# A selective scan on one core: softplus in one activation, states carried as the scan's initial value, and seven of 24 C products on GpSimd

## The chip, the core and the metric

The kernel runs on one core of a Trainium2 chip. The core has five engines, each with its own in-order queue: TensorE (PE, matmuls; PEld is its weight load), VectorE (DVE), ScalarE (ACT), GpSimd (POOL) and SyncE (SP), which here issues nearly all DMAs. They meet in the on-chip memories SBUF (128 partitions) and PSUM (TensorE's output[...]), and wait for one another through semaphores. The metric is the device time of one execution in microseconds (us), the median of several.

## What is computed

Two images of 96 channels and 128x128 pixels pass through two layers. Layer 0 normalizes over channels, adds a four-direction Mamba block, and adds a small feed-forward network (FFN); layer 1 adds a 3x3 convolution and another FFN. Nearly all time is spent in the Mamba block. For each direction, with 192 inner channels, 16 states and 16384 tokens:

```
xz = x @ in_w.T;  xc, z = split(xz)
xc = silu(causal_conv4(xc) + conv_b)
dt_raw, B, C = split(xc @ xproj_w.T)          # 6, 16, 16 columns
dt = softplus(dt_raw @ dt_w.T + dt_b)
h[t] = exp(dt[t] * A) * h[t-1] + dt[t] * B[t] * xc[t]     # per channel, 16 states
y[t] = sum_s h[t, s] * C[t, s] + Dp * xc[t]
out = (y * silu(z)) @ outp_w.T
```

The four outputs are brought back to image order, concatenated, and multiplied by `fuse_w`.

## The kernel before

For each of two images (the loop at L607) there are three stages: `normalize`, `mamba` and `ffn_and_conv`. The change touches only `mamba`.

**Tiling.** The four directions are two pairs: forward over rows with forward over columns, then the two reversed ones. One pair has 2 x 192 = 384 inner channels, that is three groups g of 128 partitions (group 1 holds half of each direction). Tokens go in tiles of T = 512, so a pair has 32 tiles; with two pairs that is 64 steps per image, 128 in all. Inside a step the states are taken two at a time: a unit is (g, s), with g in 0..2 and s in 0, 2, .., 14, which makes 24 units, numbered 0 to 23. Two neighbouring units share a four-state tile of B rows and one of C rows, called quads here: 12 of each per step.

**What a unit does.**

- ScalarE makes the decay factors: two exponentials exp(A_s * dt) of 128x512, written to PSUM (`decay`, L364).
- GpSimd multiplies a whole quad of B rows, broadcast to 128 partitions by DMA, by dt*xc, in place (`b_part`, L354). It then adds what enters this tile from the one before to the first token of each state: `enter` = exp(A * dt[first token]) * last state (L320, L357, L358).
- VectorE runs two scans along the 512 tokens, h = da*h + b, from 0.0 (L368), one instruction each.
- The scan's result is multiplied by the C rows, 128x1024, in place of C (the C product). VectorE does this for most units (L456). For the units in `BY_POOL`, (0,8), (1,0) and (1,4), GpSimd does it (L375); then the scan writes into the B tile in SBUF, which GpSimd can read, instead of the decay tile in PSUM.
- ScalarE copies the two last columns of h to `hst`, the states that the next step starts from (L457).
- TensorE adds the products over the states into one PSUM tile y per group, by matmuls with the identity (`sums`, L372). At the end of a group VectorE multiplies y by silu(z) (`gated`, L379), and `project` adds the result to the output.

**Order.** All five queues are written out by hand (`in_order`). The loop at L484 has one iteration per unit k. In it stand, in this order: at even k the DMA of the B quad of unit k+6 (`fetch`) and the `b_part` of unit k+2 (`feed`); the tasks planned for (k, 0); scan 0 of unit k; then `behind(k-1)`, with the C product, state copy and sums of the unit before; the decay factors of unit k+2; scan 1 of unit k; at even k the DMA of the C quad of unit k+4; the tasks planned for (k, 1). For a unit in `BY_POOL` the product is issued one iteration later, at (k+1, 1), and its sums three later, at (k+3, 1). B has four quad buffers, C three, the decay factors three tiles, the y tile and the `misc` tile of PSUM one each.

**The next step's preparation** is spread over the units of the current one by `prologue`: a list `at` of (unit, before or after the scans, function). It holds the input DMA, the three in-projection groups with the convolution as four shifted matmuls (`conv`), silu of xc and of z (each one activation of 128x1536 with a table load before and behind it, L261 and L262), the matmul for dt_raw, B and C (`rows`), and the dt chain of each group. That chain writes softplus(v) as max(v,0) + log(1 + exp(-|v|)) with a correction term: six activations of 128x512 on ScalarE (Abs, Relu, Exp, Identity, Ln, Identity: L291 to L302) and three 128x512 operations on GpSimd (L305, L308, L311), then dt*xc on GpSimd (`dt_u`, L315).

Of the kernel before, what the change touches and what calls it, by code (L numbers as in the profile page):

```python
# [10 lines left out]
F32 = mybir.dt.float32  # L11
# [3 lines left out]
AF = mybir.ActivationFunctionType  # L15
ALU = mybir.AluOpType
# [7 lines left out]
T = 512  # L24
NT = L // T
R = T // W
S = 16
# [4 lines left out]
NG = 3  # L32
B_AHEAD = 3
C_AHEAD = 2
AHEAD = 2
BY_POOL = ((0, 8), (1, 0), (1, 4))
BCO = 32
NBC = 4 * S

# [2 lines left out]
def tile_metaformer(ctx: ExitStack, tc: tile.TileContext, a: dict, out: bass.AP):  # L42
    nc = tc.nc

    cpool = ctx.enter_context(tc.tile_pool(name="const", bufs=1))
# [14 lines left out]
    minus_one = cpool.tile([128, 1], F32, name="minus_one")  # L60
    nc.vector.memset(minus_one, -1.0)
    ident = const("ident", (128, 128))
    acc = accp.tile([C, L], F32, name="acc")
    blk = 4 * T
# [13 lines left out]
    dtb = const("dtb", (128, 2, NG))  # L78
# [4 lines left out]
    amat = cpool.tile([128, 2, NG, S], F32, name="amat")  # L83
# [103 lines left out]
    def mamba(acc, xnr, xnc):  # L187

        with ExitStack() as st:
            pool = lambda n, bufs, **kw: st.enter_context(tc.tile_pool(name=n, bufs=bufs, **kw))  # L190

            io, gen, one, mixp, two = (pool(*p) for p in (("io", 2), ("gen", 4), ("one", 1), ("mixp", 1), ("two", 2)))
# [1 line left out]
            rows_d = pool("rows_d", 3, space=DRAM)  # L194

            hst = one.tile([128, NG, S], F32, name="hst")
            enter = one.tile([128, NG, S], F32, name="enter")
            acc_w = acc.rearrange("c (h w) -> c w h", w=W)

            def misc():  # L200
# [15 lines left out]
            def prologue(pi, i, d):  # L216

                rev = pi == 1
                lo = L - (i + 1) * T if rev else i * T
                src = []  # L220

                def load():
                    for n, dram in (("xa", xnr), ("xb", xnc)):
                        t = io.tile([C, T + 3], F32, name=n)
                        if i == 0:
                            nc.gpsimd.memset(t[:, T : T + 3] if rev else t[:, 0:3], 0.0)
                            queue = nc.sync if rev else nc.gpsimd
# [4 lines left out]
                    d["dt"], d["dtu"], d["yg"] = [], [], []  # L232

                def conv(g):
                    d["ps"] = inproj(pi, g, lambda dd, k, lo, hi: inx[:, dd, k, lo:hi], src, (0, 1, 2, 3))
# [49 lines left out]
                    w = dtw[:, pi, g * 128 : (g + 1) * 128]  # L285
                    nc.tensor.matmul(d["ps"], w, d["rows"][0 : 2 * RK, :], start=True, stop=True)

                def dt_exp(g):
                    bias = dtb[:, pi, g : g + 1]
                    e = d["e", g] = one.tile([128, T], F32, name="e")  # L290
                    nc.scalar.activation(e, d["ps"], AF.Abs, bias=bias)  # L291
                    dt = gen.tile([128, T], F32, name="dt")
                    nc.scalar.activation(dt, d["ps"], AF.Relu, bias=bias)
                    nc.scalar.activation(e, e, AF.Exp, scale=-1.0)
                    d["dt"].append(dt)

                def dt_ln(g):
                    d["q"] = one.tile([128, T], F32, name="q")
                    nc.scalar.activation(d["q"], d["e", g], AF.Identity, bias=1.0)
                    d["ln"] = one.tile([128, T], F32, name="ln")  # L300
                    nc.scalar.activation(d["ln"], d["q"], AF.Ln)
                    nc.scalar.activation(d["q"], d["q"], AF.Identity, bias=minus_one[:, 0:1])  # L302

                def dt_q(g):
                    nc.gpsimd.tensor_tensor(d["q"], d["e", g], d["q"], ALU.subtract)  # L305

                def dt_log(g):
                    nc.gpsimd.tensor_tensor(d["ln"], d["ln"], d["q"], ALU.add)  # L308

                def dt_sum(g):  # L310
                    nc.gpsimd.tensor_tensor(d["dt"][g], d["dt"][g], d["ln"], ALU.add)  # L311

                def dt_u(g):
                    dtu = gen.tile([128, T], F32, name="dtu")
                    nc.gpsimd.tensor_tensor(dtu, d["dt"][g], d["xc"][:, g, :], ALU.mult)  # L315
# [17 lines left out]
                for g, ks in enumerate(((14, 15, 16, 18), *dts)):  # L333
                    at += [(k, 0, partial(f, g)) for k, f in zip(ks, (dt_in, dt_exp, dt_ln))]
                    at += [(ks[3] - 1, 1, partial(dt_q, g))]
                    at += [(ks[3] + m, 0, partial(f, g)) for m, f in ((1, dt_log), (1, dt_sum), (2, dt_u))]
                    if i > 0:
                        at += [((20, 24, 29)[g], 1, partial(entry, g))]

                outs = (conv_out, gate_out, rows_out, dt_exp)  # L340
# [9 lines left out]
                nc.sync.dma_start(t, src[None].broadcast_to((128 // n, n, 4, T)))  # L350
                return t

            def b_part(i, d, g, s, b):
                nc.gpsimd.tensor_tensor(b, d["dtu"][g][:, None, :].broadcast_to((128, 4, T)), b, ALU.mult)  # L354
                if i > 0:
                    if s == 0:
                        nc.gpsimd.tensor_tensor(enter[:, g, :], enter[:, g, :], hst[:, g, :], ALU.mult)  # L357
                    nc.gpsimd.tensor_tensor(b[:, :, 0], b[:, :, 0], enter[:, g, s : s + 4], ALU.add)  # L358

            def decay(pi, d, g, s):  # L360

                da = ps_w.tile([128, 2, T], F32, name="da")
                for j in range(2):
                    nc.scalar.activation(da[:, j, :], d["dt"][g], AF.Exp, scale=amat[:, pi, g, s + j : s + j + 1])  # L364
                return da

            def scan(j, da, b, h):
                nc.vector.tensor_tensor_scan(h[:, j, :], da[:, j, :], b[:, j, :], 0.0, ALU.mult, ALU.add)  # L368

            def sums(s, y, c):  # L370
                for j in range(2):
# [26 lines left out]
            steps = [(pi, i) for pi in range(2) for i in range(NT)]  # L398
            units = [(g, s) for g in range(NG) for s in range(0, S, 2)]
            nu = len(units)  # L400
            total = nu * len(steps)
            state = [{} for _ in steps]
            todo = {}

            def later(k, where, rank, f, *args):
                todo.setdefault((k, where), []).append((rank, partial(f, *args)))

            def issue(k, where):
                for _, f in sorted(todo.pop((k, where), ()), key=lambda p: p[0]):
                    f()  # L410
# [17 lines left out]
            bs, cs, das, hs, quads = {}, {}, {}, {}, {}  # L428
# [8 lines left out]
            def feed(k):  # L437

                if k < total:
                    n = k // nu  # L440
                    b_part(steps[n][1], state[n], *units[k % nu], quads.pop(k))

            def feed_decay(k):
                if k < total:
# [5 lines left out]
            def behind(k):  # L450
# [3 lines left out]
                h, c = hs.pop(k), cs.pop(k)  # L454
                if (g, s) not in BY_POOL:
                    nc.vector.tensor_tensor(c, h, c, ALU.mult)  # L456
# [27 lines left out]
            for k in range(total + 6):  # L484
                n, u = divmod(k, nu)
                if u == nu - 3:

                    prepare(n + 2)
                if k % 2 == 0:
                    fetch(k + 2 * B_AHEAD, 0, B_AHEAD, bs)  # L490
                    feed(k + AHEAD)
                issue(k, 0)
                if k < total:
                    (g, s) = units[u]
                    da, b = das.pop(k), bs.pop(k)
                    hs[k] = b if (g, s) in BY_POOL else da
                    scan(0, da, b, hs[k])
                if 0 < k <= total:
                    behind(k - 1)
                feed_decay(k + AHEAD)  # L500
                if k < total:
                    scan(1, da, b, hs[k])
                if k % 2 == 0:
                    fetch(k + 2 * C_AHEAD, 1, C_AHEAD, cs)
                issue(k, 1)
# [178 lines left out]
```

## Time and profile before

| what | us |
|---|---|
| median of three runs (11809.09 to 11811.6) | 11809.75 |
| profiled execution, its span | 11811.5 |
| of it, the 128 Mamba steps, by the spacing of L379 (81.17 each) | about 10390 |
| DVE busy in one step | 79.7 |
| POOL busy in one step | 77.6 to 79.3 |
| PE busy in one step | 72.7 |
| ACT busy in one step | 61.0 |

The profile's own execution took as long as the median of the runs, so sums made against it hold for the median. The rest, some 1420 us, is the normalization, the FFN and convolution stages and the filling of the pipeline; the change leaves their code alone.

In a group line of the profile, the numbers after the bar are the total busy time, the mean duration of one instruction in ns, then how long the engine stood idle just before such instructions and what ended most of that idle time. A reported duration overlaps the next instruction a little, so costs are read from the spacing of starts. In the table by stretches of time there follow, for each engine, its busy time and in brackets the number of its instructions, then TensorE's granted clock, the share of time in which the DMA engines were busy, and GB/s.

### The profile page before, as it was taken

What the parts mean: (1) busy time and instruction counts of PE and PEld (TensorE: products, weight loads), DVE (VectorE), ACT (ScalarE), POOL (GpSimd) and SP (SyncE); (2) the same over time, 40 slices, a digit from 0 to 9 for tenths busy, and PEclk for the clock granted to TensorE, in tenths of its full rate; (3) what the DMA queues carried; (4) which work ended last, traced back from release to release, by engine and by line L of the source; (5) the groups of instructions that cost most, each with busy time, mean ns of one, the idle gap of its engine ahead of it and who ended that gap; (6) DMA issues with size and microseconds to landing.
All of it is one profiled execution on the core that took longest, in us unless ns stands there. A gap on an engine that the chain in (4) does not pass through costs nothing. (4 is left out here: it accounts for less than half of the span.)

```text
span 11811.5 us, 96408 instructions
## 1 busy us (share of the span) xinstructions
PE 10510.1 (89%) x24208; PEld 3894.5 (33%) x24208; DVE 10818.5 (92%) x10512; ACT 8548.6 (72%) x15094; POOL 10203.6 (86%) x5468
## 2 busy tenths in 40 slices
PE   7888888989888889889978888888898898888899
PEld 2333333333333333333323333333333333333333
DVE  6999999999999999994469999999999999999944
ACT  6777777777777777775567777777777777777755
POOL 5999999999999999991159999999999999999911
PEclk9999999999999999999989999999999999999999
DMA  7888888888888888880068888888888888888800
GB/s 263 323 323 324 321 327 321 320 330 318 327 324 323 324 324 321 327 317 24 26 242 319 327 324 322 324 325 320 328 320 323 328 318 327 324 323 323 319 14 13
DMA packets 540774, 3417.11 MB, mean 289 GB/s; under 512 B 67532, under 2 KB 68652, under 8 KB 143832
## 3 DMA queue, kind: packets, MB, share of 16 engines
q1 hardware_dynamic: 539960, 3410.16, 75.6%
q8 instruction: 195, 3.19, 0.1%
q14 instruction: 363, 2.97, 0.1%
q0 software_dynamic: 256, 0.79, 0.0%
HBM read 3289.04 MB, written 54.53 MB: 283 GB/s over the span
## 5 line engine op out<-in xcount | busy, mean ns | idle before, releaser
L354 POOL TENSOR_TENSOR row<-dtu,row 128x2048 f32<-128x2048 f32 x1536 | 6957.6, 4530 | 11.4 <-DMA row<-bcd 8.7
L368 DVE TENSOR_TENSOR_SCAN da<-da,row 128x512 f32<-128x512 f32 x5376 | 6324.3, 1213 | 208.0 <-ACT da L364 127.7
L372 PE MATMUL y<-row,ident 128*128 128x512 f32 x12288 | 5778.2, 604 | 667.5 <-DVE row L456 643.5
L364 ACT ACTIVATE da<-dt,amat 128x512 f32<-128x512 f32 x6144 | 4249.0, 692 | 184.3 <-POOL dt L311 1.7
L372 PEld LDWEIGHTS y<-row,ident 128*128 128x128 f32 x12288 | 2231.1, 190 | 4058.8 <-issue 2155.2
L456 DVE TENSOR_TENSOR row<-da,row 128x1024 f32<-128x1024 f32 x2688 | 3233.6, 1203 | 0.1
L457 ACT COPY hst<-da 128x2 f32<-128x2 f32 x2688 | 423.6, 158 | 2400.8 <-DVE row L456 2380.7
L213 PE MATMUL misc<-xb,inx 96*64 96x512 f32 (+1 forms) x2048 | 956.5, 610 | 130.8 <-ACT hst L457 110.4
L579 POOL TENSOR_TENSOR acc<-acc,y 96x512 f32<-96x512 f32 x128 | 147.6, 1153 | 993.9 <-DVE y L578 993.9
L368 DVE TENSOR_TENSOR_SCAN row<-da,row 128x512 f32<-128x512 f32 x768 | 927.3, 1207 | 50.6 <-ACT da L364 44.8
L213 PE MATMUL misc<-xa,inx 96*64 96x512 f32 (+1 forms) x2048 | 940.8, 602 | 27.0 <-DMA xa<-xnr 17.3
L375 POOL TENSOR_TENSOR row<-row,row 128x1024 f32<-128x1024 f32 x384 | 904.0, 2354 | 18.0 <-DVE row L368 17.1
L305 POOL TENSOR_TENSOR q<-e,q 128x512 f32<-128x512 f32 x384 | 488.5, 1272 | 261.3 <-ACT hst L457 173.4
L591 PE MATMUL pc<-pad,kw 96*96 96x512 f32 x1152 | 567.0, 593 | 0.0
L463 PE MATMUL y<-xc,dmat 128*128 128x512 f32 x768 | 421.3, 630 | 149.9 <-DVE sz L379 149.9
L311 POOL TENSOR_TENSOR dt<-dt,ln 128x512 f32<-128x512 f32 x384 | 488.6, 1272 | 30.1
L213 PEld LDWEIGHTS misc<-xa,inx 96*64 96x64 f32 (+1 forms) x2048 | 314.5, 163 | 604.2 <-issue 426.0
L315 POOL TENSOR_TENSOR dtu<-dt,xc 128x512 f32<-128x512 f32 x384 | 488.6, 1272 | 0.5
L308 POOL TENSOR_TENSOR ln<-ln,q 128x512 f32<-128x512 f32 x384 | 487.5, 1270 | 0.2
L389 PE MATMUL misc<-sz,gmat 128*96 128x512 f32 x1024 | 483.6, 594 | 0.0
L268 PE MATMUL misc<-xc,bcw 128*96 128x512 f32 x768 | 364.4, 611 | 117.6 <-ACT xc L261 91.9
L213 PEld LDWEIGHTS misc<-xb,inx 96*64 96x64 f32 (+1 forms) x2048 | 316.9, 164 | 434.1 <-issue 204.0
(82 smaller groups left out, 8926.2 us busy)
## 6 DMA issues: line engine op xcount, KB each, us to landing
row<-bcd SPq DMA_DIRECT2D x3072, 1024.0 KB, 6.4
xc<-mix SPq DMA_DIRECT2D x256, 128.0 KB, 5.4
sz<-mix SPq DMA_DIRECT2D x256, 128.0 KB, 8.4
xa<-xnr SPq DMA_DIRECT2D x124, 193.1 KB, 5.2
xb<-xnc SPq DMA_DIRECT2D x124, 193.1 KB, 5.4
bcd<-rows SPq DMA_DIRECT2D x128, 128.0 KB, 6.9
acc<-in_x_dram SPq DMA_DIRECT2D x16, 768.0 KB, 5.9
xnr<-xn SPq DMA_DIRECT2D x16, 768.0 KB, 4.3
```

The lines of the kernel that those rows point to most:

```text
L213: nc.tensor.matmul(ps[rows, :], w(PAIRS[pi][d], k, lo, hi), src[d][:, k : k + T], **se)
L305: nc.gpsimd.tensor_tensor(d["q"], d["e", g], d["q"], ALU.subtract)
L308: nc.gpsimd.tensor_tensor(d["ln"], d["ln"], d["q"], ALU.add)
L311: nc.gpsimd.tensor_tensor(d["dt"][g], d["dt"][g], d["ln"], ALU.add)
L315: nc.gpsimd.tensor_tensor(dtu, d["dt"][g], d["xc"][:, g, :], ALU.mult)
L354: nc.gpsimd.tensor_tensor(b, d["dtu"][g][:, None, :].broadcast_to((128, 4, T)), b, ALU.mult)
L364: nc.scalar.activation(da[:, j, :], d["dt"][g], AF.Exp, scale=amat[:, pi, g, s + j : s + j + 1])
L368: nc.vector.tensor_tensor_scan(h[:, j, :], da[:, j, :], b[:, j, :], 0.0, ALU.mult, ALU.add)
L372: nc.tensor.matmul(y, ident, c[:, j, :], start=False, stop=s + j == S - 1)
L375: nc.gpsimd.tensor_tensor(c, h, c, ALU.mult)
L456: nc.vector.tensor_tensor(c, h, c, ALU.mult)
L591: nc.tensor.matmul(pc, kw[:, t, :], rows, start=t == 0, stop=t == 8)
```

## The change

Three things, all in `mamba`.

1. **Softplus.** The chain is replaced by `dt_out` (Identity with the bias, PSUM to one SBUF tile for all three groups) and one activation `Softplus` over 128x1536, followed by loading the table set of exp and log again. The three GpSimd operations disappear. In the first step of an image softplus comes in two pieces. `minus_one` is no longer needed.
2. **Entering states.** `enter`, its exponential and its GpSimd operations disappear. The scan takes `hst[:, g, s:s+1]`, one value per partition in SBUF, as its initial value in all steps but the first of each pair, where it stays 0.0.
3. **C products.** `BY_POOL` becomes (0,0), (0,8), (1,0), (1,4), (1,8), (2,0), (2,8): seven units of 24 instead of three.

With the chain gone, the places of the dt tasks and of two gate tasks in the list move.

```diff
-BY_POOL = ((0, 8), (1, 0), (1, 4))
+BY_POOL = tuple((g, s) for g in range(3) for s in (0, 8)) + ((1, 4),)
...
-                def dt_exp(g):
...
-                def dt_ln(g):
...
-                def dt_q(g):
-                    nc.gpsimd.tensor_tensor(d["q"], d["e", g], d["q"], ALU.subtract)
-
-                def dt_log(g):
-                    nc.gpsimd.tensor_tensor(d["ln"], d["ln"], d["q"], ALU.add)
-
-                def dt_sum(g):
-                    nc.gpsimd.tensor_tensor(d["dt"][g], d["dt"][g], d["ln"], ALU.add)
+                def dt_out(g):
+                    if g == 0:
+                        d["dt"] = two.tile([128, NG, T], F32, name="dt")
+                    nc.scalar.activation(d["dt"][:, g, :], d["ps"], AF.Identity, bias=dtb[:, pi, g : g + 1])
+
+                def softplus(lo, hi):
+                    t = d["dt"][:, lo:hi, :]
+                    nc.scalar.activation(t, t, AF.Softplus)
+                    nc.scalar.preload_act_table_set("natural_log_exp_and_others")
...
-                def entry(g):
-
-                    nc.scalar.activation(enter[:, g, :], amat[:, pi, g, :], AF.Exp, scale=d["dt"][g][:, 0:1])
...
-                for g, k in ((1, 7), (0, 17), (2, 21)):
+                for g, k in ((1, 7), (0, 18), (2, 21)):
                     at += [(k, 0, partial(gate, g)), (k + 1, 0, partial(gate_out, g))]
-                dts = ((24, 25, 26, 27), (31, 32, 33, 35)) if first else ((18, 19, 20, 22), (22, 23, 24, 26))
...
+                soft = ((0, 1, 16), (1, 3, 26)) if first else ((0, 3, 17),)
+                for x0, x1, k in soft:
+                    at += [(k, 1, partial(softplus, x0, x1))]
+                for g, k in enumerate((14, 24, 25) if first else (14, 15, 16)):
+                    at += [(k, 0, partial(dt_in, g)), (k + 1, 0, partial(dt_out, g))]
+                for g, k in enumerate((19, 27, 29)):
+                    at += [(k, 0, partial(dt_u, g))]
...
-            def b_part(i, d, g, s, b):
+            def b_part(d, g, s, b):
                 nc.gpsimd.tensor_tensor(b, d["dtu"][g][:, None, :].broadcast_to((128, 4, T)), b, ALU.mult)
-                if i > 0:
-                    if s == 0:
-                        nc.gpsimd.tensor_tensor(enter[:, g, :], enter[:, g, :], hst[:, g, :], ALU.mult)
-                    nc.gpsimd.tensor_tensor(b[:, :, 0], b[:, :, 0], enter[:, g, s : s + 4], ALU.add)
...
-            def scan(j, da, b, h):
-                nc.vector.tensor_tensor_scan(h[:, j, :], da[:, j, :], b[:, j, :], 0.0, ALU.mult, ALU.add)
+            def scan(i, g, s, da, b, h):
+                j = s % 2
+                start = hst[:, g, s : s + 1] if i > 0 else 0.0
+                nc.vector.tensor_tensor_scan(h[:, j, :], da[:, j, :], b[:, j, :], start, ALU.mult, ALU.add)
```

More of the change, by code (lines that the diff above doesn't have):

```diff
@@ L59, in tile_metaformer @@
     nc.vector.memset(eps_t, 1e-5)
-    minus_one = cpool.tile([128, 1], F32, name="minus_one")
-    nc.vector.memset(minus_one, -1.0)
     ident = const("ident", (128, 128))
@@ L196, in mamba @@
             hst = one.tile([128, NG, S], F32, name="hst")
-            enter = one.tile([128, NG, S], F32, name="enter")
             acc_w = acc.rearrange("c (h w) -> c w h", w=W)
@@ L231, in load @@
                         src.append(t[:, ::-1] if rev else t)
-                    d["dt"], d["dtu"], d["yg"] = [], [], []
+                    d["dtu"], d["yg"] = [], []
                 def conv(g):
@@ L286, in dt_in @@
                     nc.tensor.matmul(d["ps"], w, d["rows"][0 : 2 * RK, :], start=True, stop=True)
-                def dt_exp(g):
[L289 to L295, printed above, removed]
-                def dt_ln(g):
[L298 to L302, printed above, removed]
-                def dt_q(g):
-                    nc.gpsimd.tensor_tensor(d["q"], d["e", g], d["q"], ALU.subtract)
-                def dt_log(g):
-                    nc.gpsimd.tensor_tensor(d["ln"], d["ln"], d["q"], ALU.add)
-                def dt_sum(g):
-                    nc.gpsimd.tensor_tensor(d["dt"][g], d["dt"][g], d["ln"], ALU.add)
+                def dt_out(g):
[6 more added lines that the diff above has]
+                    nc.scalar.preload_act_table_set("natural_log_exp_and_others")
                 def dt_u(g):
                     dtu = gen.tile([128, T], F32, name="dtu")
-                    nc.gpsimd.tensor_tensor(dtu, d["dt"][g], d["xc"][:, g, :], ALU.mult)
+                    nc.gpsimd.tensor_tensor(dtu, d["dt"][:, g, :], d["xc"][:, g, :], ALU.mult)
                     d["dtu"].append(dtu)
-                def entry(g):
-                    nc.scalar.activation(enter[:, g, :], amat[:, pi, g, :], AF.Exp, scale=d["dt"][g][:, 0:1])
                 first = pi == 0 and i == 0
@@ L329, in prologue @@
                     at += [(k, 0, partial(conv, g)), (k + 1, 1, partial(conv_out, g))]
-                for g, k in ((1, 7), (0, 17), (2, 21)):
+                for g, k in ((1, 7), (0, 18), (2, 21)):
                     at += [(k, 0, partial(gate, g)), (k + 1, 0, partial(gate_out, g))]
-                dts = ((24, 25, 26, 27), (31, 32, 33, 35)) if first else ((18, 19, 20, 22), (22, 23, 24, 26))
[L333 to L336, printed above, removed]
-                    if i > 0:
-                        at += [((20, 24, 29)[g], 1, partial(entry, g))]
-                outs = (conv_out, gate_out, rows_out, dt_exp)
+                soft = ((0, 1, 16), (1, 3, 26)) if first else ((0, 3, 17),)
[5 more added lines that the diff above has]
+                    at += [(k, 0, partial(dt_u, g))]
+                outs = (conv_out, gate_out, rows_out, dt_out)
                 at = [(k, where, getattr(f, "func", f) not in outs, f) for k, where, f in at]
@@ L351, in row_tile @@
                 return t
-            def b_part(i, d, g, s, b):
+            def b_part(d, g, s, b):
                 nc.gpsimd.tensor_tensor(b, d["dtu"][g][:, None, :].broadcast_to((128, 4, T)), b, ALU.mult)
-                if i > 0:
-                    if s == 0:
-                        nc.gpsimd.tensor_tensor(enter[:, g, :], enter[:, g, :], hst[:, g, :], ALU.mult)
-                    nc.gpsimd.tensor_tensor(b[:, :, 0], b[:, :, 0], enter[:, g, s : s + 4], ALU.add)
             def decay(pi, d, g, s):
@@ L363, in decay @@
                 for j in range(2):
-                    nc.scalar.activation(da[:, j, :], d["dt"][g], AF.Exp, scale=amat[:, pi, g, s + j : s + j + 1])
+                    nc.scalar.activation(da[:, j, :], d["dt"][:, g, :], AF.Exp, scale=amat[:, pi, g, s + j : s + j + 1])
                 return da
-            def scan(j, da, b, h):
-                nc.vector.tensor_tensor_scan(h[:, j, :], da[:, j, :], b[:, j, :], 0.0, ALU.mult, ALU.add)
+            def scan(i, g, s, da, b, h):
+                j = s % 2
+                start = hst[:, g, s : s + 1] if i > 0 else 0.0
+                nc.vector.tensor_tensor_scan(h[:, j, :], da[:, j, :], b[:, j, :], start, ALU.mult, ALU.add)
             def sums(s, y, c):
@@ L440, in feed @@
                     n = k // nu
-                    b_part(steps[n][1], state[n], *units[k % nu], quads.pop(k))
+                    b_part(state[n], *units[k % nu], quads.pop(k))
             def feed_decay(k):
@@ L496, in mamba @@
                     hs[k] = b if (g, s) in BY_POOL else da
-                    scan(0, da, b, hs[k])
+                    scan(steps[n][1], g, s, da, b, hs[k])
                 if 0 < k <= total:
@@ L501, in mamba @@
                 if k < total:
-                    scan(1, da, b, hs[k])
+                    scan(steps[n][1], g, s + 1, da, b, hs[k])
                 if k % 2 == 0:
```

## The prediction

> **What bounds the kernel now.** I first read the costliest groups, to see which engine has the work:
>
> ```profile
> L354 POOL TENSOR_TENSOR row<-dtu,row 128x2048 f32<-128x2048 f32 x1536 | 6957.6, 4530 | 11.4 <-DMA row<-bcd 8.7
> L368 DVE TENSOR_TENSOR_SCAN da<-da,row 128x512 f32<-128x512 f32 x5376 | 6324.3, 1213 | 208.0 <-ACT da L364 127.7
> L456 DVE TENSOR_TENSOR row<-da,row 128x1024 f32<-128x1024 f32 x2688 | 3233.6, 1203 | 0.1
> L375 POOL TENSOR_TENSOR row<-row,row 128x1024 f32<-128x1024 f32 x384 | 904.0, 2354 | 18.0 <-DVE row L368 17.1
> ```
>
> DVE's scans and products idle almost nowhere. Second, one Mamba step by stretches of time (from one `gated` to that 24 units later; columns as above):
>
> ```profile
> 2011.83:2093.00 81.17, 72.66 (x168) 26.85 (x166) 79.68 (x74) 61.02 (x108) 78.60 (x43) 1.00 0.84 324
> ```
>
> DVE is busy 79.68 of 81.17 us, POOL 78.60, PE 72.66, ACT 61.02, DMA 84%. Two engines are nearly full; which one sets the pace is told by the third view, who waited for whom on DVE:
>
> ```profile
> DVE da L368 <- ACT da L364: 127.7, 126, 1.0
> ...
> DVE da L368 <- POOL row L354: 71.4, 2, 35.8
> ...
> DVE row L368 <- ACT da L364: 44.8, 112, 0.4
> ```
>
> Its two waits for POOL are the pipeline fills of the two images. So DVE sets the pace. Per step it loses 1.4 us: 0.4 and 1.0 us behind the two silu, whose load, activation and load (1.28 + 1.48 + 1.28 us) delay decay factors. Fourth, DVE's order of time, for spacing:
>
> ```profile
> 2028.27 2.33 DVE L368 TENSOR_TENSOR_SCAN da<-da,row 128x512 f32<-128x512 f32 x2
> 2030.51 1.20 DVE L456 TENSOR_TENSOR row<-da,row 128x1024 f32<-128x1024 f32 x1
> 2031.63 1.22 DVE L368 TENSOR_TENSOR_SCAN da<-da,row 128x512 f32<-128x512 f32 x1
> 2032.76 1.20 DVE L368 TENSOR_TENSOR_SCAN row<-da,row 128x512 f32<-128x512 f32 x1
> 2033.87 1.20 DVE L456 TENSOR_TENSOR row<-da,row 128x1024 f32<-128x1024 f32 x1
> ```
>
> A scan or a product takes 1.12 us from start to start; about 0.09 of its reported 1.21 overlaps the next. A step is 48 scans + 21 products = 69 x 1.12 = 77.3, three `gated` at 0.60 = 1.8, waits 1.4: 80.5 of 81.17.
>
> **What the Trainium skill says.** "VectorE: DVE Perf Modes", Scalar operands: a scalar is an immediate or a [P, 1] operand; it gives no price for the second, so I take that from the trace. "ScalarE: Activation LUTs", What ACT_TABLE_LOAD costs: a load takes about 1283 ns, as here (L261: 1283). "SBUF — State Buffer", Who interferes with whom: a DVE instruction with at most one SBUF input, outside two-port modes, does not contend with GpSimd. That fits: scans and products have one SBUF operand and keep 1.12 us beside a nearly full POOL. Whether the pointed-to scalar counts as a second input it does not say, and no row of before shows it.
>
> **The change, part by part.**
>
> *C products.* 4 x 128 = 512 products leave DVE: 512 x 1.12 = **-573 us**. POOL gains 512 x 2.31 (spacing of L375) = 1183.
>
> *Softplus.* POOL loses 3 x 384 operations of 1.27: -1463, plus `enter`'s 1488 x 0.20 and 372 x 0.22: -385. POOL per step is then 12 x 4.48 + 7 x 2.31 + 3 x 1.24 = 73.7, under DVE's. The tightest place is group 1, with POOL products at units 8, 10 and 12: POOL needs 2.31 + 4.48 = 6.8 us per quad, DVE 4 x 1.17 + 1.12 = 5.8, or 6.4 with a `gated`. Counted from the end of scan 1 of unit 8, POOL finishes the B quads of units 12, 14 and 16 at 6.8, 13.6 and 20.4 us; DVE wants them at 8.7, 14.5 and 21.4 (scans 1.17, products 1.12, one `gated` 0.6, no wait counted). The least cover is 0.9 us, at unit 14; each us that POOL were later beyond it would cost 128. ACT per step loses six 128x512 activations per group (L291 to L302, 3.94 us a set: 11.8) and three `enter` exponentials (0.9); it gains three Identity like L241 (2.0) and loads plus softplus at silu's 4.05: 54 of 79 us. The softplus stands after unit 17's decay factors: ACT is held 4.05 us, and the factors of unit 20 follow it. From the end of scan 1 of unit 16 they are ready after 1.6 (state copy, factors of 19) + 4.05 + 1.7 (state copy, factors of 20) = 7.3 us; DVE wants them after six scans, two products and a `gated`, 7.0 + 2.24 + 0.6 = 9.8. It is hidden with 2.5 us to spare; an uncovered us would cost 128. Behind it on POOL waits only dt*xc at unit 19, due 5.7 us after that scan, which POOL reaches at 6.8.
>
> *Initial value.* 5952 scans (124 of 128 steps x 48) get a [128,1] operand; the state copy is 24 units old, so no wait arises. The nearest rows are DVE's TENSOR_SCALARs:
>
> ```profile
> 40.80 0.21 DVE L103 TENSOR_SCALAR amat<-alog 128x96 f32<-128x96 f32 x1 [1.68 <-ACT alog L102]
> 40.93 0.68 DVE L138 TENSOR_TENSOR xn<-xm,rs 96x512 f32<-96x512 f32 x1
> 41.53 0.66 DVE L108 TENSOR_SCALAR dmat<-ident,dskip 128x128 f32<-128x128 f32 x3
> 42.11 0.68 DVE L138 TENSOR_TENSOR xn<-xm,rs 96x512 f32<-96x512 f32 x1
> ```
>
> L103 has an immediate: 0.13 us start to start for 96 columns. L108 has a pointer: 0.58/3 = 0.193 for 128. If both run at two columns per 0.96 GHz cycle, as I estimate from the skill's first page above (fp32 `tensor_scalar` 2x; 50 and 67 ns), the fixed parts are 80 and 126: the pointer costs 46 ns. Single durations (209 and 274) give 48. Bounds: 0, if the scan loads it under its predecessor; 109, ScalarE's difference between L302 (722, bias pointer) and L299 (613, immediate); and, if the overlap of 90 ns is lost too, 46 + 90 = 136. I take 46: L108's three keep 0.08 us of overlap. 5952 x 0.046 = **+274 us**.
>
> *Small terms.* Scans that are 46 ns longer give ACT five times that before each silu-delayed scan: 0.23 x 2 x 128 = **-58**. New on PE: `sums` of unit 12 now come right before dt_in and those of unit 15, which `gated` waits for. After the product of unit 14, PE has 1.72 + 1.72 + 0.86 + 1.72 + 0.2 = 6.25 us to do and DVE 5.85 before `gated`; with hand-off, 0.5 per step, **+64**. Fill: before the first scan ACT and POOL need 4.7 us less twice: **-9**. C quads with a POOL product are given back by PE two units later; seven instead of three of 12 quads per step have this. SP's C loads already wait for PE:
>
> ```profile
> SPq L350 <- PE y L372: 4709.3, 1529, 17.4
> ```
>
> DVE nonetheless never waits for a DMA; C quads have about 13 us, 6.3 of it transfer. I cost it at nothing, and what it costs if that slack is gone is rival 3.
>
> Sum: 11811.5 - 573 + 274 - 58 + 64 - 9 = **11509.5**, 78.8 per step (PE 92%, DMA 86%). The profiled time equals the median, so I predict 11510.
>
> **The rivals.**
>
> 1. *The pointed-to initial value breaks the overlap (slower).* 136 ns per scan: 5952 x 0.136 = 809; both silu waits shrink by at most 0.41 and 0.68, -140; total 11811 - 573 + 809 - 140 + 64 - 9 = 11962. For: how a scan starts up with such an operand is shown nowhere in the trace; contention with POOL over it would land here too, or worse. Against: L108's spacing. The time is the old one at about 107 ns (5952 x 0.107 = 637, silu -121, other terms -518), slower from there on.
> 2. *The pointer is free.* 11510 - 274 + 58 (the silu waits stay) = 11294, or 11235 if PE's wait is absent too. For: a fixed 53 ns per scan (1120 - 1067) may hold it. Against: L108 and L103.
> 3. *Buffers: the B and C quads come back late*, SP is held, POOL or DVE then waits for rows. For: SP's 4709 us on PE, 17.4 at longest; DMA at 86%. Against: POOL waits 8.7 us for rows in the whole run. With four more such quads per step at 0.5 us each: 2 x 128 = 256, total 11766.
> 4. *POOL takes the bound over.* Its products wait for a DVE scan and its next B quad stands behind them, so it can't work ahead. For: 73.7 us of work in a step of 78.8. Against: the cover worked out above. It would need 7.5 us of idle POOL per step to end at the old time, 11811; at half of it, 81.17 - 3.75 = 77.4, DVE still sets the pace.
>
> **Chances.** Main case 0.48 (11400 to 11640: pointer 30 to 60 ns, small waits up to 0.6 us per step); free pointer 0.12; late buffers 0.16, most still faster; overlap lost or worse 0.22; POOL as the bound, ending between the main case and the old time, 0.02. No change means within 0.2%, 24 us, about what a measurement of this kernel can tell. Faster 0.48 + 0.12 + 0.12 = 0.72; same 0.04; slower 0.22 + 0.02 = 0.24. The range of 8 in 10 takes part of the free pointer below and reaches toward the lost overlap above: 11290 to 11980.
>
> **What would show it.** Scans of DVE at about 1.17 us spacing in steps after a pair's first and 1.12 in its first; 2176 products at 1203 on DVE and 896 at 2354 on POOL; POOL near 74 us of a 79 us step; 768 table loads beside exponentials instead of 512; DVE's waits for ACT at two places per step, shorter, none behind softplus; a new DVE wait for PE of about 0.5 us at `gated` of group 1. Wrong: scan spacing over 1.21; DVE waiting for POOL or for DMA; the step not ending on DVE.

## The result and the profile after

The changed kernel takes 11736.62 us (median of 4 runs, 11729.43 to 11739.88), against 11809.42 before (median of the 4 runs beside it): ratio 0.9936 with the interval 0.9922 to 0.995. It is faster by 73 us; 302 were forecast (11811.5 to 11509.5). The sign was right and the time lies inside the range, but three quarters of the gain are missing, and the experiments below look for those 229 us. The forecast's main case (11400 to 11640) did not come about. The profiled execution spans 11738.1 us.

First the costliest groups of the changed kernel (instruction, shape, count | busy us, mean ns of one | idle before and what ended it):

```profile
L330 POOL TENSOR_TENSOR row<-dtu,row 128x2048 f32<-128x2048 f32 x1536 | 6940.4, 4522 | 460.4 <-DMA row<-bcd 460.2
L342 DVE TENSOR_TENSOR_SCAN da<-da,hst,row 128x512 f32<-128x512 f32 x4216 | 5267.4, 1277 | 106.0 <-ACT da L336 88.5
L430 DVE TENSOR_TENSOR row<-da,row 128x1024 f32<-128x1024 f32 x2176 | 2622.3, 1205 | 7.8 <-DMA row<-bcd 6.5
L349 POOL TENSOR_TENSOR row<-row,row 128x1024 f32<-128x1024 f32 x896 | 2110.3, 2355 | 402.9 <-DVE row L342 285.1
```

512 products have left DVE (2688 to 2176) and stand on POOL (896) with unchanged durations. A scan that names `hst` is reported at 1277 ns, where one before was 1213. POOL's B products now wait 460 us for their rows (8.7 before), while DVE's wait for rows is only 6.5.

Second, one step by stretches of time, from one `gated` to that 24 units later (us; busy time of PE, PEld, DVE, ACT, POOL, with counts; PE clock, DMA share, GB/s):

```profile
2129.67:2210.28 80.61, 73.32 (x166) 27.59 (x166) 78.39 (x68) 55.13 (x94) 73.88 (x23) 0.98 0.84 326
```

POOL's 73.88 is the 73.7 of the sum, ACT's 55.13 the 54. But the step is 80.61 us and not 78.8, and DVE is busy 78.39 of it, though it has 4 x 1.12 = 4.5 us of products less to do. Third, DVE's waits (us in total, times, longest):

```profile
DVE sz L353 <- PE y L346: 182.9, 251, 3.1
DVE da L342 <- ACT da L336: 95.8, 128, 1.8
...
DVE row L342 <- POOL row L330: 88.1, 4, 43.1
```

The waits for ACT behind the silu have shrunk from 172.5 to 95.8, and there is none behind the softplus. The wait of `gated` for PE is new: 182.9 us in 251 places, nearly two per step, where the kernel before has

```profile
DVE sz L379 <- PE y L372: 24.8, 4, 10.7
```

By the start times, 115.1 of the 182.9 stand at `gated` of group 1, 45.4 at group 0 and 24.0 at group 2, there in a dozen scattered steps. The pipeline fill, the last line of the three, was 71.4 (in 2 places). Fourth, DVE in order of time at `gated` of group 1 (start us, us from first start to last end, instruction, count, idle before it):

```profile
2044.17 1.20 DVE L430 TENSOR_TENSOR row<-da,row 128x1024 f32<-128x1024 f32 x1
2045.28 1.28 DVE L342 TENSOR_TENSOR_SCAN row<-da,hst,row 128x512 f32<-128x512 f32 x1
2046.47 1.27 DVE L342 TENSOR_TENSOR_SCAN da<-da,hst,row 128x512 f32<-128x512 f32 x1
2048.65 0.69 DVE L353 TENSOR_TENSOR sz<-y,sz 128x512 f32<-128x512 f32 x1 [0.91 <-PE y L346]
2049.26 2.46 DVE L342 TENSOR_TENSOR_SCAN da<-da,hst,row 128x512 f32<-128x512 f32 x2
2051.62 1.21 DVE L430 TENSOR_TENSOR row<-da,row 128x1024 f32<-128x1024 f32 x1
```

From 2045.28 to 2046.47 is 1.19 us for a scan; from 2049.26 to 2051.62 two take 2.36, 1.18 each. In the kernel before it was 1.12. The `gated` is late by 0.91 us. PE in the same stretch:

```profile
2041.94 3.70 PE L346 MATMUL y<-row,ident 128*128 128x512 f32 x8
2045.58 1.12 PE L283 MATMUL misc<-rows,dtw 12*128 12x512 f32 x2
2046.63 1.98 PE L346 MATMUL y<-row,ident 128*128 128x512 f32 x4
```

These are the sums of units 14 and 12 (eight matmuls), dt_in, and the sums of unit 15, which `gated` needs. They end at 2048.61, and `gated` starts at 2048.65. The granted clock of TensorE was 1.00 in this stretch.

### The profile page after: what moved, and what is told of

It is laid out like the page before. It is cut to its first block, busy times and chain, and to the rows that moved or that the text cites. A ratio compares the mean times of both kernels' runs of the same rounds, so it can differ in the third digit from the quotient of the medians.

```text
span 11738.1 us, 92994 instructions
## 1 busy us (share of the span) xinstructions
PE 10500.3 (89%) x24208; PEld 3959.1 (34%) x24208; DVE 10636.2 (91%) x9999; ACT 7800.1 (66%) x13192; POOL 9611.9 (82%) x2968
## 5 line engine op out<-in xcount | busy, mean ns | idle before, releaser
L330 POOL TENSOR_TENSOR row<-dtu,row 128x2048 f32<-128x2048 f32 x1536 | 6940.4, 4522 | 460.4 <-DMA row<-bcd 460.2
L342 DVE TENSOR_TENSOR_SCAN da<-da,hst,row 128x512 f32<-128x512 f32 x4216 | 5267.4, 1277 | 106.0 <-ACT da L336 88.5
L346 PEld LDWEIGHTS y<-row,ident 128*128 128x128 f32 x12288 | 2273.3, 192 | 3987.4 <-issue 2294.6
L430 DVE TENSOR_TENSOR row<-da,row 128x1024 f32<-128x1024 f32 x2176 | 2622.3, 1205 | 7.8 <-DMA row<-bcd 6.5
L349 POOL TENSOR_TENSOR row<-row,row 128x1024 f32<-128x1024 f32 x896 | 2110.3, 2355 | 402.9 <-DVE row L342 285.1
L431 ACT COPY hst<-da 128x2 f32<-128x2 f32 x2176 | 348.4, 160 | 3009.4 <-DVE row L430 3007.9
L342 DVE TENSOR_TENSOR_SCAN row<-da,hst,row 128x512 f32<-128x512 f32 x1736 | 2201.4, 1268 | 1.2 <-ACT hst L431 0.7
L283 PE MATMUL misc<-rows,dtw 12*128 12x512 f32 x768 | 434.3, 645 | 40.5 <-ACT dt L288 37.8
L361 PE MATMUL misc<-acc,ident 96*96 96x512 f32 x512 | 389.9, 847 | 82.7 <-ACT sz L246 54.0
L136 DVE TENSOR_TENSOR xq<-xm,rs 96x512 fp8e5<-96x512 f32 x128 | 87.9, 687 | 387.6 <-ACT rs L132 387.6
```

Source lines behind the costliest of these rows:

```text
L346: nc.tensor.matmul(y, ident, c[:, j, :], start=False, stop=s + j == S - 1)
L349: nc.gpsimd.tensor_tensor(c, h, c, ALU.mult)
```

## The experiments

The kernel before was timed again beside each of these kernels; its medians lie between 11809.26 and 11812.22, and each ratio is against the one beside it. Spacings (start to start) are medians over all such neighbours, worked out from the start times of the instructions in the trace.

**Initial value alone.** The kernel before, with `entry`, `enter` and POOL's operations on it left out and

```
...
-                nc.vector.tensor_tensor_scan(h[:, j, :], da[:, j, :], b[:, j, :], 0.0, ALU.mult, ALU.add)
...
+                start = hst[:, g, s : s + 1] if i > 0 else 0.0
+                nc.vector.tensor_tensor_scan(h[:, j, :], da[:, j, :], b[:, j, :], start, ALU.mult, ALU.add)
```

> The initial value from hst alone, on the kernel before. Theory (the pointed-to initial value costs each scan 0.065 us of start-to-start time, as the trace after suggests): 5952 x 0.065 = +387, less what the two waits behind silu give back (five longer scans each, 0.33 x 2 x 126 = -82): about 12110, slower. Rival (the price is the 0.046 us of the prediction and the rest of the lost gain went into new waits that the seven products bring): +274 - 58, about 12025. In both GpSimd gets idle time and nothing else changes.

Measured: 12095.22 us, 1.0243 (1.0227 to 1.0258), 286 more. Two of its groups of scans, with the operand and, in a pair's first step, without:

```profile
L359 DVE TENSOR_TENSOR_SCAN da<-da,hst,row 128x512 f32<-128x512 f32 x5208 | 6433.8, 1271 | 95.7 <-ACT da L353 87.0
L359 DVE TENSOR_TENSOR_SCAN da<-da,row 128x512 f32<-128x512 f32 x168 | 198.1, 1214 | 76.2 <-POOL row L347 71.8 <-ACT da L353 4.0
```

Inside one kernel, on the same tiles, the pointed-to scalar lengthens a scan from 1214 to 1271 ns. By spacing, a scan before a product goes from 1.115 to 1.175 us and a scan before a scan from 1.127 to 1.188: 60 ns. 5952 x 0.060 = 357; the waits behind silu give back 58 (172.5 to about 115), so 299 were to come of it, and 286 did. So the operand has a fixed price of 60 ns, above the 46 forecast, and this part of the change by itself makes the kernel slower. The overlap of neighbours stays, so rival 1 is out, and so is rival 2.

**First-token entry kept.** The changed kernel with the softplus and the seven products, but with `enter` as before, scans from 0.0:

```
-                start = hst[:, g, s : s + 1] if i > 0 else 0.0
...
+                if i > 0:
+                    if s == 0:
+                        nc.gpsimd.tensor_tensor(enter[:, g, :], enter[:, g, :], hst[:, g, :], ALU.mult)
+                    nc.gpsimd.tensor_tensor(b[:, :, 0], b[:, :, 0], enter[:, g, s : s + 4], ALU.add)
```

> The changed kernel with its entering states by the first token again (scans from 0.0): softplus and seven products alone. Theory: 387 us come back, of which the two silu waits take about 80; the waits for TensorE at gated stay at 1.3 us per step or grow a little: 11738 - 387 + 80 = about 11430. GpSimd then has 73.7 + 2.8 = 76.5 us of work per step of 78.1, so DVE waits for it here and there; if GpSimd becomes the bound, 11500 or more. Rival with 0.046 us: 11738 - 274 + 58 = about 11520 without any wait for GpSimd.

Measured: 11554.08 us, 0.9782 (0.9766 to 0.9799): faster by 255. It misses 11430 by 124. POOL has 76.57 us of work in a step of 79.34 and DVE 75.85, so both are nearly full; DVE waits for PE at `gated` (143.0 in 198 places), for POOL's products (about 60), and for rows (52.3 in 106, against 6.5 in the changed kernel). The last two are small forms of rivals 4 and 3. At `gated` of group 0 the view names a copy on ACT in 53 more places (35.5 us), but there too PE's last sum ends 0.107 us before `gated` starts, as in the places that it puts down to PE; counted as PE's they make 178.5. Undoing the initial value gains 183 us, about half of the 357 by which the scans are shorter.

**Softplus alone.** That kernel with the old three products on POOL.

```
-BY_POOL = tuple((g, s) for g in range(3) for s in (0, 8)) + ((1, 4),)
+BY_POOL = ((0, 8), (1, 0), (1, 4))
```

> Softplus alone: entering states by the first token, products as before. Theory: GpSimd was not the bound, so its 11.5 us per step of freed time bring nothing; ScalarE's are off the path as well: 11800 to 11830, with 5 to 10 us more at the start of each image. Rival (a softplus of 4 us on ScalarE delays decay factors): DVE waits for ScalarE at a third place per step, 0.5 us or more each, 11875 or more.

Measured: 11807.05 us, 0.9998 (0.9989 to 1.0006): no change. POOL's time freed became waiting for rows (660.7 us) and for DVE; ACT held by the softplus delayed no scan (DVE's waits for ACT stand at the same two places of a step as before, units 10 and 13, both behind a silu). As costed, this part is worth nothing but room on POOL.

**Products alone.** The opposite edit: the kernel before with the new `BY_POOL` and nothing else.

> Seven products on GpSimd alone, softplus chain and first-token entry as before. Theory (DVE sets the pace only as long as GpSimd has room, and softplus makes that room): GpSimd gets 78.6 + 4 x 2.31 = 87.8 us of work per step, becomes the bound: 11810 + 128 x 6.7 = about 12670 or more, DVE waits for B quads. Rival (GpSimd's work doesn't matter): 11810 - 573 + 130 = about 11370.

Measured: 12761.69 us, 1.0807 (1.0791 to 1.0823). Its step is 88.84 us, of which POOL is busy 87.67, and DVE waits for POOL:

```profile
DVE row L368 <- POOL row L358: 920.8, 500, 2.9
DVE da L368 <- POOL row L358: 422.1, 316, 1.5
```

Seven products without the softplus overload POOL. The two parts need each other: alone they bring 0 and +952, together (the kernel with entry kept) -255.

**Softplus and initial value, without the products.** The changed kernel with the old `BY_POOL`.

> Softplus and the initial value without the products: the changed kernel with the three old units on GpSimd. Theory (the parts add up, and the initial value costs 0.060 us per scan with or without the chain): 11807 + 286 = about 12093; the four products per step then bring 12093 - 11737 = 356 us of the forecast 573. Rival (with GpSimd's chain gone the initial value costs less, because what it cost was contention with a full GpSimd): 12020 or less.

Measured: 12100.78 us, 1.0246 (1.0229 to 1.0263). That is the initial value alone (12095.22) within 6 us, with the same spacings of scans, 1.174 and 1.187, though POOL is busy 78% of the time here and 91% there (from 2500 to 4500 us of the trace). From this kernel to the changed one is the effect of the four more products with the other two parts in place: 12100.78 - 11736.62 = 364 us, where the sum had 512 x 1.12 = 573. So 209 us of the products' gain are lost, and the suspect is the wait for PE at `gated`, 182.9 us in the changed kernel and here

```profile
DVE sz L353 <- PE y L346: 4.2, 2, 2.1
```

It comes with the products, not with the other two parts.

**The sums of one unit earlier.** `later(k + 3, ...)` queues on PE the sums of a unit whose product POOL makes. For unit 12 alone they go two units later and so stand before those of unit 14, not behind:

```
-                    later(k + 3, 1, True, sums, s, y, c)
+                    later(k + (2 if (g, s) == (1, 8) else 3), 1, True, sums, s, y, c)
```

> The changed kernel with the sums of unit 12 one iteration earlier (k+2 in place of k+3), so that they no longer stand right before those of unit 15. Theory (it is this place in TensorE's queue that gated of group 1 waits for): the wait of 0.91 us per step at the end of group 1 goes, the 0.2 to 0.4 us at the end of group 0 stay; 11737 - 126 x 0.95 = about 11615. Rival (TensorE, busy 72.4 of 80.5 us, is short of time as such): the wait moves to another gated and the time stays above 11700.

Measured: 11650.33 us, 0.9862 (0.9846 to 0.9879), 86 less than the changed kernel. The waits at `gated` fall from 182.9 to

```profile
DVE sz L353 <- PE y L346: 102.9, 239, 3.1
```

80 us less for 86 less of time: this wait is on the path that sets the end, almost one for one. It was 0.91 us at group 1 and is now 0.38 there; the other half of what is left stands at group 0.

**All of POOL's sums two units later.** `k + 2` for every such unit.

> The same for all seven units with a GpSimd product. Theory: the waits at the ends of groups 0 and 1 go, 158 us over the run and 0.09 us of lost overlap with each of 251: about 11560; C quads also come back earlier, so SyncE's waits for TensorE and GpSimd's 460 us for B rows shrink, which alone brings nothing. Rival (TensorE short of time as such): above 11700.

Measured: 11615.72 us, 0.9834 (0.9819 to 0.9849), 121 less than the changed kernel.

```profile
DVE sz L353 <- PE y L346: 56.0, 130, 2.1
```

127 us of waits less for 121 of time. Group 0's have gone with the sums of unit 4, which stood before it as those of unit 12 do before group 1's; 0.4 us at group 1 stays. C buffers come back a unit sooner as well: SP's wait for PE falls from 6736 to 5380 us, and the 460 us of POOL's wait for rows are gone. Their going brings nothing beyond the 127, so POOL's waits for rows were covered. (They are larger, 660.7 and 1019.3 us, in the two kernels with the softplus and only three products on POOL, where POOL has more time to spare; their size is no measure of late buffers.) TensorE's granted clock is no rival for these differences: it was 0.982 over the changed kernel, 0.990 with the sums of unit 12 moved and 0.979 here, where the waits are shortest.

**Entry kept and sums two later.** Both edits, the initial value undone.

> Softplus, seven products, entering states by the first token, sums two iterations later: TensorE's waits and the pointed-to initial value both gone. Theory: 11554 - 143 (waits for TensorE) = about 11420, if GpSimd, with 76.5 us of work per step, keeps up; each us per step that it doesn't costs 128. Rival (GpSimd is the bound there already): 11500 or more, DVE's waits for GpSimd growing by what those for TensorE lose.

Measured: 11436.98 us, 0.9682 (0.9668 to 0.9697): faster than the kernel before by 375 us and than the changed one by 300. One step, and the wait at `gated`:

```profile
2045.79:2124.17 78.38, 72.69 (x167) 27.95 (x167) 75.44 (x69) 55.78 (x97) 76.56 (x38) 0.98 0.88 335
```

```profile
DVE sz L363 <- PE y L356: 222.3, 252, 2.1
```

Here undoing the initial value gains 11615.72 - 11436.98 = 179 us, though the scans are shorter by 357: the waits for PE rise by 166 (56.0 to 222.3) and those behind silu from 96.3 to 133.9. The faster DVE runs into PE, which has 72.69 us of work in 78.38. Against the first kernel with entry kept it gains 117 us. DVE's waits for POOL's products and for rows, about 110 us, are gone, and those at `gated` grow by 44 (178.5 to 222.3); 266 waits fewer, each with some 0.09 us of overlap lost (below), are about 24 more. The rest, some 27 us, was not separated.

**Six products on POOL, two placements.** The same with units 0 and 4 of a group (states 0 and 8), and with 2 and 4 (states 4 and 8):

```
+BY_POOL = tuple((g, s) for g in range(3) for s in (0, 8))
```

> As the one before, with six products on GpSimd: (1,4) goes back to DVE. Balance by spacing per step: DVE 75.7 us, GpSimd 74.2, against 74.6 and 76.5 with seven. Theory (DVE sets the pace with its waits for ScalarE of 1.4 us and 0.7 us of rest): 77.8 us per step, 11380. Rival (GpSimd is not the bound with seven): 143 us slower than with seven.

Measured: 11541.49 us, 0.9771 (0.9756 to 0.9785), 104 more than with seven: one product fewer moved is 128 x 1.12 = 143, DVE's waits for decay factors fell by 129 (133.9 to 4.5), and those at `gated` grew by 88, to

```profile
DVE sz L363 <- PE y L356: 310.2, 252, 3.9
```

My reading was that `gated` of a group comes after the product of the next group's first unit in DVE's queue, so that a product moved from there takes 1.12 us out of DVE's stretch before `gated`, and leaves PE as much less time for its sums. So the next kernel puts them elsewhere:

```
+BY_POOL = tuple((g, s) for g in range(3) for s in (4, 8))
```

> As e8 (softplus, first-token entry, six products on GpSimd, sums two later), with the six at (g,4) and (g,8) in place of (g,0) and (g,8). Theory (a GpSimd product at s = 0 takes away the DVE product that stood between the last product of a group and its gated, so TensorE has 1.12 us less for the last sums): the 310 us of waiting for TensorE at gated fall to about 25, with 0.09 us of overlap for each; three more pairs of dependent scans per step stand next to each other at 0.12 us each, +46: about 11280. Rival (TensorE, busy 93%, is short of time as such): the waits stay or move, 11450 or more.

Measured: 11606.57 us, 0.9828 (0.9811 to 0.9844). The waits at `gated` did fall, and two others came in their place:

```profile
DVE da L352 <- ACT da L347: 138.1, 129, 5.1
DVE da L352 <- POOL row L341: 137.1, 183, 1.6
DVE sz L363 <- PE y L356: 67.1, 68, 3.2
```

310.2 - 67.1 = 243 us less for PE, but 275 in the two other lines, which were 4.5 with the placement before. The expectation (11280) failed: it counted a wait as saved which only moved.

**Seven, placed late.** States 4 and 8 of each group and state 0 of group 1, and dt*xc of group 2 two units later.

```
+BY_POOL = tuple((g, s) for g in range(3) for s in (4, 8)) + ((1, 0),)
...
+                for g, k in enumerate((19, 27, 31)):
```

> The same with (1,0) as a seventh, and dt*xc of group 2 two units later so that it does not stand between two GpSimd products. Theory: DVE gains 1.12 us per step less a wait for TensorE at the end of group 0 of 0.5 to 1 us; GpSimd, with 76.5 us of work, is now as full as DVE: about 11250, the best version. If GpSimd is the bound: DVE waits for B rows, 11300 or more.

Measured: 11484.59 us, 0.9725 (0.971 to 0.9739), not the best: 48 more than with the placement of the change. DVE waits for ACT 134.4, for POOL 82.0, and at `gated`:

```profile
DVE sz L363 <- ACT hst L441: 100.0, 124, 1.2
```

The view puts this down to the state copy, but it is PE's wait: PE's last sum ends 0.107 us before `gated` starts, as at group 0 of the changed kernel, where the view names PE. It stands at group 0 alone, 0.82 us per step, as the expectation had it (0.5 to 1); group 1, whose next unit's product is on DVE again, waits no more. That bears out the reading above, though not wholly: with the placement before, `gated` of group 1 waits in 66 steps (60.8 of the 67.1 us) in spite of that product. What the expectation missed is that the waits for POOL came with it, and that those for ACT stayed.

## Why the prediction came out as it did

**What it had right.** The sign, and the bound: DVE set the pace before and sets it after. 512 products left it, at an unchanged 1.12 us; POOL is not full (73.88 of 80.61); the softplus is hidden and alone worth nothing (0.9998). Loads of the activation tables rose from 512 to 772: 768, and four for the two first steps whose softplus comes in two pieces. The silu waits shrank as scans grew longer. Of the late C quads, POOL's waits for rows (8.7 to 460.2 us, gone when the sums come sooner) may be a sign; DVE they did not reach (6.5). That supports the decision to cost it at nothing, for this kernel only: with shorter scans DVE did wait 52 us for rows.

That the time lies inside the range of 11290 to 11980 is owed to luck: the range reached up for a lost overlap, which did not happen. The main case asked for a pointer of 30 to 60 ns and new waits of up to 0.6 us per step; the pointer came at its upper edge and the wait for PE at 1.4 us per step (182.9/128). Two sums of the prediction are slightly off, without effect: its five terms for PE add to 6.22 and not 6.25, and rival 2 without PE's wait comes to 11230 and not 11235.

**What failed: terms of the sum.** In us, with each measured value from the waits or the spacings above:

| step of the prediction | forecast | measured |
|---|---|---|
| C products leave DVE, 512 x 1.12 | -573 | -573 |
| initial value, 5952 x 46 ns | +274 | +357 (60 ns) |
| silu waits shrink | -58 | -77 |
| new wait for PE at `gated` | +64 | +158 |
| fill | -9 | +17 |
| overlap lost, 0.09 a wait: 247 more for PE, 106 fewer for ACT | none | +13 |
| scans that have become neighbours, 256 x 0.13 | none | +34 |
| sum | -302 | -71 |

The measured change is -73, closer than the rounded terms can promise.

*Initial value, mis-sized by 83.* The 46 ns came from two TENSOR_SCALAR rows and an estimate of their throughput. The scan alone, inside one kernel, gives 60. The form of the step held (a fixed price per instruction, no lost overlap, hidden by nothing), and the direct bounds of 0 and 136 contained it. The step "the silu waits give back five times the added length" held at the longer of the two waits: 0.29 us each time with the initial value alone (127.7 to 91.0 us in all), for 5 x 0.060. The shorter one, 44.8 us before, kept 23.5 there and is gone in the changed kernel; so some 20 of the 77 come with the products, and the step is not to be credited with them.

*The wait for PE, mis-sized by 94.* The place was right and the cause in the main: the sums of unit 12 stand ahead of what `gated` of group 1 needs, and moving them away gave 86 us and took 0.52 of the 0.91 us there; 0.38 stays with them gone. The size was 0.91 us at group 1 instead of 0.5. The prediction counted 6.25 us of PE against 5.85 of DVE; in the trace PE's run from the product of unit 14 to the end of the sums of unit 15 takes about 6.7: eight sums 3.64 from start to start instead of 3.44, dt_in 1.05 instead of 0.86, the last four sums 1.98 to their end instead of 1.72. And the sum was made only for group 1. `gated` of group 0 waits as well, mostly 0.43 us, behind the sums of unit 4. Those stood there before too, without a wait; what is new is that DVE has one product less in group 0 (unit 0's), which I take for the cause without having tried it alone.

*Fill, the wrong sign.* DVE's wait for POOL's first rows grew from 71.4 to 88.1, not by the promised -9. In the trace ACT's first `mix` waits for a DMA that stores `xnc` and starts at 96.75 us instead of 86.29. All the kernels with the softplus have this longer fill. Why the DMA comes later (where the tiles lie in memory, for one) was not tried.

*Lost overlap, not foreseen.* A waiting instruction starts after the end of the one before it. In DVE's order of time above, the scan at 2046.47 is followed by `gated` 2.18 us later, where a `gated` that does not wait follows after 1.18: 1.00 more for an idle time of 0.91. The missing 0.09 is in no line of waits. Each wait for ACT that went away gave the same amount back: in the kernel before, one of 0.41 us made 1.63 out of a spacing of 1.13.

*Neighbouring scans, not foreseen.* In the order of the queue the product of a unit stands between the two scans of the next unit. Where POOL makes it, these two follow each other directly, and four scans stand in a row. By the start times, from the second of the four to the third (the two of one unit) it is 1.307 us instead of 1.188 in the changed kernel (1.240 instead of 1.127 in the one before), and from the third to the fourth 1.200. Such places grew from 256 to 512: 256 x (0.119 + 0.012) = 34 us. In one such place of the changed kernel the first stands at 2059.70, and behind it are

```profile
2060.89 3.78 DVE L342 TENSOR_TENSOR_SCAN da<-da,hst,row 128x512 f32<-128x512 f32 x3
2064.58 1.21 DVE L430 TENSOR_TENSOR row<-da,row 128x1024 f32<-128x1024 f32 x1
```

that is 3.69 us for three scans, where 3 x 1.18 would be 3.54. The trace's records of semaphores say more than this view, which leaves out idle times under 150 ns: the third of the four carries a wait for VectorE's own semaphore, and the engine idles 35 ns before it, until the scan in front has ended (260 places in the kernel before, 532 in the changed one). With the 0.09 of overlap lost that makes the 0.12. So a wait of one scan for the one before it in its own unit is in the trace; no run took it away.

The losses that come with the products are 179 (182.9 - 4.2) of waits for PE, 34 of neighbours and 12 of overlap, less 27 by which waits for ACT shrank (124.6 to 97.4). That makes 198, where the run without the products showed 209; the attribution holds to that accuracy.

**The rivals.** Lost overlap: out, by the spacing of 1.18. Free pointer: out, by 1271 against 1214. Late buffers: at most seen on POOL, without effect on the time. POOL as the bound: out here, and shown to be the end of the same change without the softplus (+952). None of the worked-out times was near 11737 for its own reason; those of rivals 3 and 4 (11766, 11811) stand closer than the main case, but their mechanisms did not set the time.

**What the change left on the table.** Its first part makes room on POOL, its third uses it, and its second costs more on DVE (357) than the operations that it takes off POOL could have cost there: with these kept, POOL has 76.56 us of work in a 78.38 us step and the kernel ends at 11437.

## What to carry to other kernels

Work moved off the engine that sets the pace is paid in full only as long as the next engine is on time; go through every place where the pacing engine waits for another, not only the one that the new order touches, because each becomes tighter by the time just saved. An operand that costs 60 ns a time is dear when it stands in 5952 instructions of the full engine, and the work that it takes off an engine with slack is worth less (without it DVE waited some 112 us for POOL's products and for rows, against 357 of longer scans); measure such an operand in its own instruction rather than from a neighbour's. When a wait is removed by a new placement, ask which engine had been covered by it: here the later placement of six passed the wait from PE on to ACT and POOL, and the later one of seven passed on a part of it. And when a view puts a wait down to something that the instruction does not need, see what else ended just before: the state copy at `gated` was PE.

## What the hardware showed that was not expected

A [128, 1] tile as initial value of a scan of 128x512 adds 60 ns from start to start (1.115 to 1.175 us ahead of a product, 1.127 to 1.188 ahead of a scan), and leaves the overlap of some 0.09 us with the next instruction in place. It is the same with POOL busy 78% of the time (1.187 in the kernel with three products there) and 92% (1.188 in the changed kernel). Inside the former, scans ahead of a product take 1.174 us both in the 317 places where POOL is idle all through the scan and in the 1900 where it is busy all through it, so no contention of the two engines for the memory shows. The Trainium skill's "SBUF — State Buffer", Who interferes with whom, left open whether such a scalar counts as a second SBUF input; these spacings give no sign that it does. And four scans in a row without a product between cost more than their number: one of the gaps is 1.240 us instead of 1.127 with the scan from 0.0, and 1.307 instead of 1.188 with the pointer, at the scan that waits for VectorE's own semaphore. A wait costs more than the idle time that a profile shows: 0.09 us of overlap goes with it, at the 0.91 us of `gated` as at these 35 ns.
